# A Mamba-2 block with eight LoRA experts on one NeuronCore: turning h and B by VectorE squares and DRAM in place of TensorE transposes

## The chip, the cores and the metric

The kernel runs on one NeuronCore of a Trainium2 chip. A core has TensorE (PE in the profile), VectorE (DVE), ScalarE (ACT), GpSimd (POOL) and SyncE (SP), which here issues every DMA. The metric is the device time of one execution in microseconds (us). The kernel before took 1603.26 us, the median of three runs (1601.43 to 1604.12).

## The reference

The input x has 1024 rows (time steps) of 512. It is normalised, and three things are added up: x, a Mamba-2 block of the normalised x, and a dense layer with a top-2 mixture of eight rank-16 LoRA experts.

```python
proj = einsum('bsd,ed->bse', xn, in_proj_w)          # gate 8192, hBC 10240, dt 128
hBC  = silu(causal_conv4(hBC) + conv_b)              # hs: 128 heads x 64; B, C: 8 groups x 128
dt   = clip(softplus(dt + dt_bias), 0, 100)
xch  = hs * dt                                       # in chunks of 128 steps
A_cum = cumsum(dt * -exp(A_log))                     # in each chunk
Y_diag = einsum('bzlhn,bzshn,bhzls,bzshp->bzlhp', C, B, L, xch)    # L = exp(segsum), lower triangle
states = einsum('bzlhn,bhzl,bzlhp->bzhpn', B, decay_states, xch)   # handed on from chunk to chunk
Y_off  = einsum('bzlhn,bzhpn,bhzl->bzlhp', C, prev, exp(A_cum))
g = (Y_diag + Y_off + hs * D) * silu(gate)
out = einsum('bsi,oi->bso', group_rms_norm(g) * norm_w, out_proj_w)
```

All is float32. Large products are computed as three matmuls of numbers split in a high and a low part (hi x hi, hi x lo, lo x hi).

## The kernel before

**Stage 1.** The normalised x lies turned in SBUF (channels on partitions, time along the row) as xh and xl. The 18,432 output channels of the projection, and the 128 of dt, are computed in 145 blocks of 128 channels by 1024 steps. `block` (L664) loads a weight (wr, 256 KB), splits it (ACT makes wh, POOL makes wl, `split` L323), and `project` (L407) runs 24 matmuls of 128x512 into two PSUM banks (pp_r). ACT and DVE take these out: a gate block through Silu, the others through four conv taps (L685, L694) and Silu (L697). Results have channels on partitions.

The scan works on units of four heads, that is, two blocks of h (`scan`, L739; 32 units, four to a group). Some products need time on partitions, so h and B have to be turned:

- `group` (L706) turns B by 8 PE transposes (bt, L718), from whose PSUM banks ACT and DVE make the split parts bh and bl (L720, L722). It also makes cbm, the masked product of C and B (cb, L732).
- `scan` turns each of the two h blocks by 8 PE transposes in two halves of time (hT, L776). DVE multiplies each half by dt (xdt, L778), POOL by the decay (xf, L784), and ACT and POOL split that (xdh L789, xdl L791).
- Three matmuls per chunk make the states' increments (ps, L802); DVE runs the recurrence over chunks (st, L809 and L813).
- For each head a row of A_cum is loaded to all partitions (L, 512 KB); ACT and DVE make of it the decay matrix (L758, L760, L762). Two products of half the array's width follow: yo from st and C (L837), y from xdt and L (L849). DVE and POOL combine them with h, D and the gate (L841 to L859), and the result is stored in DRAM (g_d).

**Stage 2.** The experts and the dense layer (`ffn`, L507; pp_rt, pp_la, pf) stand between; then the gated result is loaded again by time (gr), split, and multiplied with the output weights (po, L920); the norm is applied to the sums (L941).

**Order.** No loop of the source sets the order of instructions. Every operation is handed to a planner (`Plan`, L98) with an engine, a duration, what it reads and writes, and an urgency: its unit's number plus an offset from the table URGE. The planner plays the engines through and gives each engine, when free, the ready operation with the lowest number, and each buffer a place when it is first needed. CAPS says how many buffers of a kind may live at once; PSUM is eight banks shared by the kinds mm, ts and yy. For PE it also charges changes between the kinds of matmul (SHORT, LONG, HALVES for y and yo, MIDDLE for ps). Instructions are then written in that order, and every engine, and SP with its DMAs, executes its own in order.

Of the kernel before, what the change touches and what calls it, by code (L numbers as in the profile page):

```python
# [8 lines left out]
F32 = mybir.dt.float32  # L9
FR = mybir.dt.float32r  # L10
AF = mybir.ActivationFunctionType
ALU = mybir.AluOpType
# [37 lines left out]
URGE = dict(w=9.24, part=-0.279, proj=-0.002, evac=-1.876, silu=-2.632, group=-0.486, hT=0.407, xdt=2.385, xf=-1.176,  # L50
            split=-0.323, ps=-2.368, st=-1.089, Ll=-7.231, Lr=6.458, Le=2.863, Lm=5.964, el=-2.393, yo=0.086,
            tt=-1.918, y=3.42, yt=-3.901, out=1.039, switch=2.019, short=0.042, long=0.133, halves=-1.335,
            middle=-3.841, leave=2.869, c0=36.517, c=0.019, ffn=32.348, rt=-5.457, la=-0.436, early=-6.249,
            hold=0.232, gate=-0.092, w0=79.012)
CAPS = dict(hs=5, gate=15, ct=2, L=7, e=2, xdt=25, wr=3, wh=3, wl=8, y=4, tt=2, xf=2, mm=13, ts=3, yy=17)
# [42 lines left out]
class Plan:  # L98
# [33 lines left out]
    def run(self):  # L132
# [11 lines left out]
        while left:  # L144
            began = False
            soon = 1e30
            for e in ENGINES:
# [4 lines left out]
                for o in todo[e]:  # L152
                    same = e == "PE" and o.mode == mode == HALVES
                    if o.ready > t + 1e-9:
                        soon = min(soon, o.ready)
                        stay |= same and o.ready < t + URGE["hold"]
                        continue
# [3 lines left out]
                    if e == "PE" and o.mode != mode:  # L161
                        urge += URGE[("short", "long", "halves", "middle")[o.mode]]
                        if mode == HALVES:
                            urge += URGE["leave"]
# [10 lines left out]
                    for k, bs in wanted.items():  # L175
# [12 lines left out]
                        if ready[many[pool] - 1] > t + 1e-9:  # L188
                            soon = min(soon, ready[many[pool] - 1])
                            stay |= same and ready[many[pool] - 1] < t + URGE["hold"]  # L190
                            good = False
                            break
# [50 lines left out]
def block_kernel(ctx, tc, x, in_w, conv_w, conv_b, dt_bias, A_log, Dv, norm_w, out_w,  # L243
# [10 lines left out]
    def ctile(shape, name, dt=F32):  # L254
# [19 lines left out]
    elast_d = dram.tile([H, NZ], F32, name="elast_d")  # L274
    g_d = [dram.tile([BPG, P, S], F32, name=f"g_d{g}") for g in range(G)]
# [5 lines left out]
    big, wide, small = Pool("big", 30, 1024, sb), Pool("wide", 3, 1792, sb), Pool("small", 15, 512, sb)  # L281
    K = {n: Kind(big, CAPS.get(n, 1)) for n in ("hs", "gate", "bT", "ct", "cbm", "bh", "bl", "L", "e", "xdt", "dts", "As",
                                                "dec", "eA")}
# [19 lines left out]

    def halves(h):
        return slice(h * HALF, (h + 1) * HALF)
# [11 lines left out]
    XH, XL = new("xh", "xh", S, FR), new("xl", "xl", S, FR)  # L317
    G_D = [thing(f"g_d{g}") for g in range(G)]
# [18 lines left out]
    op("PE", 6.0, warm_up(12), w=[warm], urge=-9.0)  # L337
# [5 lines left out]
    for n, what in enumerate((0, 1, wdt, 2, 3, w0, 4, 5, 6, 7)):  # L343
        lag, urge = 2.64 + (0.3, 0.38)[n > 2] * n + 0.1 * (n > 2), -8.0 + 0.001 * n
# [16 lines left out]
    split(*wdt, -7.3)  # L361
# [45 lines left out]
    def project(w, acc, half, urge, take=(), quarters=False):  # L407

        for q in range(2) if quarters else ():
            def go(q=q):  # L410
                n, c = 0, slice(q * 256, q * 256 + 256)
                hi, lo = w[0](), w[1]()
                for a, b in ((hi, XH()), (hi, XL()), (lo, XH())):
                    for k in range(NK):
                        pe.matmul(acc()[:, c], a[:, k, :], b[:, k, halves(half)][:, c], start=n == 0, stop=n == 11)
                        n += 1
            mk = 3 << 4 * half + 2 * q
            op("PE", 1.44, go, r=[w[0], w[1], (XH, mk), (XL, mk)], w=[(acc, 1 << q)], urge=urge,
               take=take if q == 0 else (), mode=LONG)
# [244 lines left out]
    def block(u, i, row, ci, kind, name):  # L664
# [3 lines left out]
        if row:  # L668
            dma(raw, lambda: in_w[row], 3.6, w=[raw], urge=urge + URGE["w"])
            split(raw, hi, lo, urge + URGE["part"])  # L670
# [34 lines left out]

    def group(g, u):  # L706
# [5 lines left out]
        for hf in range(2):  # L712
            zs = slice(hf * 4, hf * 4 + 4)
            acc = new("mm", f"bt{g}_{hf}", P)

            def turn(acc=acc, hf=hf):
                for z4 in range(4):
                    pe.transpose(acc()[:, z4, :], gr.B()[:, zsl(hf * 4 + z4)], ident)  # L718
            op("PE", 0.436, turn, r=[gr.B], w=[acc], urge=urge, take=[gr.bh, gr.bl] if not hf else ())
            op("ACT", 0.49, lambda acc=acc, zs=zs: act.activation(gr.bh()[:, zs, :], acc(), AF.Copy), r=[acc],  # L720
               w=[(gr.bh, zmask(hf))], urge=urge)
            op("DVE", 0.6, lambda acc=acc, zs=zs: dve.tensor_tensor(  # L722
                gr.bl()[:, zs, :], acc(), f32(gr.bh()[:, zs, :]), ALU.subtract), r=[acc, (gr.bh, zmask(hf))],
                w=[(gr.bl, zmask(hf))], urge=urge)
# [14 lines left out]
    def scan(u, hs, gate):  # L739
# [24 lines left out]
        for j in range(2):  # L764
            b = 2 * u + j
            cols = slice(j * P, (j + 1) * P)
            for hf in range(2):
                tp = new("ts", f"hT{b}_{hf}", P)
                n = 4 - hf
                zs4, zs = slice(hf * 4, hf * 4 + 4), slice(hf * 4, hf * 4 + n)  # L770
                mk = zmask(hf)
                late = 0.02 * (2 * j + hf)

                def turn(tp=tp, hf=hf, j=j):
                    for z4 in range(4):
                        pe.transpose(tp()[:, z4, :], hs[j]()[:, zsl(hf * 4 + z4)], ident)  # L776
                op("PE", 0.436, turn, r=[hs[j]], w=[tp], urge=at("hT") + late, take=[xdt[j]] if not hf else ())
                op("DVE", 0.6, lambda tp=tp, j=j, b=b, zs4=zs4: dve.tensor_tensor(  # L778
                    xdt[j]()[:, zs4, :].rearrange("p z (a c) -> p z a c", a=2),
                    tp().rearrange("p z (a c) -> p z a c", a=2),  # L780
                    dts()[:, zs4, 2 * b:2 * b + 2].unsqueeze(3).to_broadcast([P, 4, 2, 64]), ALU.mult),
                    r=[tp, dts], w=[(xdt[j], mk)], urge=at("xdt") + late)
                xf = new("xf", f"xf{b}_{hf}", shape=[P, n, P])
                op("POOL", 1.0 if n == 4 else 0.8, lambda xf=xf, j=j, b=b, zs=zs, n=n: pool.tensor_tensor(  # L784
                    xf().rearrange("p z (a c) -> p z a c", a=2),
                    xdt[j]()[:, zs, :].rearrange("p z (a c) -> p z a c", a=2),
                    dec()[:, zs, 2 * b:2 * b + 2].unsqueeze(3).to_broadcast([P, n, 2, 64]), ALU.mult),
                    r=[(xdt[j], mk), dec], w=[xf], urge=at("xf") + late, port=True)
                op("ACT", 0.54 if n == 4 else 0.44, lambda xf=xf, zs=zs, cols=cols: act.activation(  # L789
                    xdh()[:, zs, cols], xf(), AF.Copy), r=[xf], w=[(xdh, mk << 8 * j)], urge=at("split") + late)  # L790
# [200 lines left out]
```

## Time and profile before

| | us |
|---|---|
| median of three runs (lowest, highest) | 1603.26 (1601.43, 1604.12) |
| the profiled execution | 1604.36 |
| its span, first to last instruction | 1602.7 |
| PE projection matmuls (pp_r, L426), share of the chain | 45% |
| PE output matmuls (po, L920), share of the chain | 22% |
| PE hT (L776), share of the chain | 3% |
| DVE xdt from PSUM (L778), 128 of 512 wide | 80.2 busy, 683 ns each |
| ACT table loads, 203 in all | 1283 ns each |
| DMA, mean over the span | 143 GB/s, 229.98 MB |

The profile comes from one execution, and its times are compared with that execution's own. "Busy" is time in which an engine has an instruction running; on PE these records overlap. The chain is found from the last instruction backwards: at each step to what released it, or to the instruction before it on its engine. The granted clock (PEclk) is 1.00 after the first 50 us.

### The profile page before, as it was taken

How to read it: one execution, taken by the hardware profiler on the slowest of the kernel's cores; microseconds unless marked ns; L12 is line 12 of the kernel's file. 1: busy time of each engine (PE TensorE's matmuls, PEld its weight loads, DVE VectorE, ACT ScalarE, POOL GpSimd, SP SyncE). 2: the span in 40 equal slices, each digit the busy share in tenths (PEclk: the TensorE clock that was granted, in tenths of full speed). 3: DMA queues.
4: the chain of work that ended last, by engine and by line, in shares of the span. 5: the costliest groups of instructions: out<-in, count | busy, mean ns of one | idle time of the engine just before them, and what ended most of it. 6: DMA issues, size and time to landing. Idle time of an engine off the chain costs nothing.

```text
span 1602.7 us, 28828 instructions
## 1 busy us (share of the span) xinstructions
PE 1592.1 (99%) x10616; PEld 1355.2 (85%) x10616; DVE 1282.2 (80%) x2209; ACT 1294.4 (81%) x2275; POOL 832.9 (52%) x768
## 2 busy tenths in 40 slices
PE   8999999999999999999999999999999999999999
PEld 8888888888888888888888888888887888888887
DVE  6798987786888788777878877787788788888874
ACT  6899989997999899799989988998973554444531
POOL 3269757847775776678576847866755000000000
PEclk9999999999999999999999999999999999999999
DMA  4534725444443555344344615544545655554512
GB/s 132 186 105 155 244 89 175 136 136 135 148 154 117 172 158 162 108 161 155 116 138 146 204 66 157 183 155 129 155 135 173 169 139 156 158 142 127 138 55 72
DMA packets 140605, 229.98 MB, mean 143 GB/s; under 512 B 11056, under 2 KB 76720, under 8 KB 140464
## 3 DMA queue, kind: packets, MB, share of 16 engines
q1 hardware_dynamic: 140464, 228.14, 46.5%
q8 instruction: 84, 1.38, 0.4%
q14 instruction: 57, 0.47, 0.1%
HBM read 191.39 MB, written 36.70 MB: 142 GB/s over the span
## 4 chain that ended last, share of the span: by engine, by line
PE 93%; POOL 3%; ACT 2%; issue 1%; DMA 0%; DVE 0%; SPq 0%; POOLq 0%; DVEq 0%
PE pp_r L426 45%; PE po L920 22%; PE y L849 7%; PE yo L837 6%; PE ps L802 5%; PE hT L776 3%; PE pf L652 1%; PE cb L732 1%; POOL yt L856 1%; POOL xdl L791 1%; POOL xf L784 1%; ACT L L758 1%; POOL g L859 1%; PE bt L718 0%; PE vp L932 0%
## 5 line engine op out<-in xcount | busy, mean ns | idle before, releaser
L426 PE MATMUL pp_r<-xh,wh 128*128 128x512 f32 x1144 | 454.2, 397 | 0.0
L426 PE MATMUL pp_r<-xh,wl 128*128 128x512 f32 x1144 | 446.3, 390 | 1.3 <-POOL wl L325 1.3
L426 PE MATMUL pp_r<-xl,wh 128*128 128x512 f32 x1144 | 446.4, 390 | 0.0
L694 DVE SCALAR_TENSOR_TENSOR h<-pp_r,cw,h 128x512 f32<-128x512 f32 (+2 forms) x384 | 283.3, 748 | 73.7 <-ACT h L685 67.7
L758 ACT ACTIVATE L<-L,As 128x128 f32<-128x128 f32 x1024 | 319.4, 391 | 0.0
L325 POOL TENSOR_TENSOR wl<-wr,wh 128x512 fp32r<-128x512 f32 x144 | 192.4, 1340 | 208.3 <-ACT wh L324 182.8
L426 PEld LDWEIGHTS pp_r<-xh,wl 128*128 128x128 f32 x1144 | 214.8, 188 | 48.3 <-POOL wl L325 2.2
L426 PEld LDWEIGHTS pp_r<-xh,wh 128*128 128x128 f32 x1144 | 215.0, 188 | 45.7 <-issue 3.9
L426 PEld LDWEIGHTS pp_r<-xl,wh 128*128 128x128 f32 x1144 | 215.2, 188 | 41.0
L762 DVE TENSOR_TENSOR L<-L,cbm 128x1024 f32<-128x1024 f32 x128 | 189.0, 1493 | 52.5 <-ACT L L760 52.1
L910 ACT ACTIVATE gr<-gr 128x1024 f32<-128x1024 f32 x64 | 67.8, 1060 | 157.6 <-DVE gl L908 157.6
L856 POOL TENSOR_TENSOR yt<-yt,tt 128x384 f32<-128x384 f32 (+1 forms) x128 | 157.3, 1240 | 68.8 <-DVE yt L853 60.4
L859 POOL TENSOR_TENSOR g<-yt,g 128x512 f32<-128x512 f32 x128 | 185.2, 1458 | 3.1
L791 POOL TENSOR_TENSOR xdl<-xf,xdh 128x512 fp32r<-128x512 f32 (+1 forms) x128 | 152.3, 1198 | 28.1 <-ACT xdh L789 28.1
L784 POOL TENSOR_TENSOR xf<-xdt,dec 128x512 f32<-128x512 f32 (+1 forms) x128 | 131.8, 1040 | 55.8 <-DVE xdt L778 55.6
L813 DVE SCALAR_TENSOR_TENSOR st<-st,eA,ps 128x64 f32<-128x64 f32 x768 | 151.4, 276 | 1.1
L911 DVE TENSOR_REDUCE sq<-gr 128x128 f32<-128x1024 f32 x64 | 128.7, 2013 | 19.1 <-ACT gr L910 19.0
L760 ACT ACTIVATE L<-L 128x1024 f32<-128x1024 f32 x128 | 135.6, 1059 | 1.5
L920 PE MATMUL po<-owh,gh 128*128 128x512 f32 x512 | 128.9, 394 | 0.0
L778 DVE TENSOR_TENSOR xdt<-hT,dts 128x512 f32<-128x512 f32 x128 | 80.2, 683 | 59.7 <-PE hT L776 59.7
L920 PE MATMUL po<-owh,gl 128*128 128x512 f32 x512 | 126.5, 389 | 0.0
L920 PE MATMUL po<-owl,gh 128*128 128x512 f32 x512 | 126.5, 389 | 0.0
(175 smaller groups left out, 2806.1 us busy)
## 6 DMA issues: line engine op xcount, KB each, us to landing
L<-acum_d SPq DMA_DIRECT2D x128, 512.0 KB, 5.8
wr<-in_w SPq DMA_DIRECT2D x144, 256.0 KB, 2.8
g_d<-g SPq DMA_DIRECT2D x64, 512.0 KB, 4.6
gr<-g_d SPq DMA_DIRECT2D x64, 512.0 KB, 6.7
e<-exp_d SPq DMA_DIRECT2D x128, 224.0 KB, 6.3
ow<-out_w SPq DMA_DIRECT2D x64, 256.0 KB, 3.6
x<-x SPq DMA_DIRECT2D x8, 256.0 KB, 5.3
acc<-x SPq DMA_DIRECT2D x8, 256.0 KB, 4.3
```

The costliest lines, as they stand in the source:

```text
L325: op("POOL", dur[1], lambda: pool.tensor_tensor(lo(), raw(), f32(hi()), ALU.subtract), r=[raw, hi], w=[lo], urge=urge, port=True)
L426: pe.matmul(acc(), a[:, k, :], b[:, k, halves(half)], start=n == 0, stop=n == 11)
L694: dve.scalar_tensor_tensor(d, acc()[:, :n], cw[:, ci, k:k + 1], d, ALU.mult, ALU.add)
L758: act.activation(L()[:, z, :], L()[:, z, :], AF.Relu, bias=As()[:, z, h:h + 1], scale=-1.0)
L760: op("ACT", 0.97, lambda L=L: act.activation(L(), L(), AF.Exp, scale=-1.0), w=[L], urge=at("Le") + 0.05 * a, table="exp")
L762: op("DVE", 1.14, lambda L=L: dve.tensor_tensor(L(), L(), gr.cbm(), ALU.mult), r=[gr.cbm], w=[L], urge=at("Lm") + 0.05 * a, port=True)
L784: op("POOL", 1.0 if n == 4 else 0.8, lambda xf=xf, j=j, b=b, zs=zs, n=n: pool.tensor_tensor(xf().rearrange("p z (a c) -> p z a c", a=2), x ...
L791: op("POOL", 1.24 if n == 4 else 0.96, lambda xf=xf, zs=zs, cols=cols: pool.tensor_tensor(xdl()[:, zs, cols], xf(), f32(xdh()[:, zs, cols] ...
L813: dve.scalar_tensor_tensor(st()[:, z, c], st()[:, z - 1, c], eA()[:, 4 * u + a, z:z + 1], pt()[:, z % 2, c], ALU.mult, ALU.add)
L856: op("POOL", 1.25 if n == 4 else 0.97, lambda yt=yt, tt=tt, part=part: pool.tensor_tensor(yt()[:, part], yt()[:, part], tt()[:, part], ALU ...
L859: op("POOL", 1.24, lambda yt=yt, j=j, hf=hf: pool.tensor_tensor(gate[j]()[:, halves(hf)], yt(), gate[j]()[:, halves(hf)], ALU.mult), r=[yt ...
L920: pe.matmul(po(), a()[:, b, :], wts[g, b // per][k]()[:, b % per, :], start=n == 0, stop=n == 23)
```

## The change

In the changed kernel no transposes of h and B are made on PE. A new function `turn` does it: DVE's transpose instruction turns each 32x32 square of a 128x1024 block, four DMAs store the result in one of four 512 KB places in DRAM so that the squares change their partitions, and one DMA loads it back. ACT and DVE then read bh and bl, and xdt, from this SBUF tile (moved), not from PSUM. xdt, xf, xdh and xdl are now cut by head (64 columns, all eight chunks) and no longer by half of time, and ps and y wait for whole tiles.

The buffers are shared out anew (34 large ones in place of 30), the urgencies are new, the planner's charge for a change of matmul kind becomes a table of pairs, the loads at the start stand in another order, and the first projections are handed over in smaller pieces. A reserve for DMAs issued by GpSimd, which the kernel has none of, is cut to 512 bytes.

```diff
-CAPS = dict(hs=5, gate=15, ct=2, L=7, e=2, xdt=25, wr=3, wh=3, wl=8, y=4, tt=2, xf=2, mm=13, ts=3, yy=17)
+CAPS = dict(hs=4, gate=4, ct=2, L=6, e=4, xdt=9, turned=5, wr=4, wh=3, wl=9, y=2, tt=1, xf=4, mm=5, ts=9, yy=5)
...
                     if e == "PE" and o.mode != mode:
-                        urge += URGE[("short", "long", "halves", "middle")[o.mode]]
-                        if mode == HALVES:
-                            urge += URGE["leave"]
+                        urge += URGE["SLHM"[mode] + "SLHM"[o.mode]]
...
+    turn_d = [dram.tile([4, 32, 4, 256], F32, name=f"turn_d{i}") for i in range(4)]
...
-    big, wide, small = Pool("big", 30, 1024, sb), Pool("wide", 3, 1792, sb), Pool("small", 15, 512, sb)
+    big, wide, small = Pool("big", 34, 1024, sb), Pool("wide", 3, 1792, sb), Pool("small", 15, 512, sb)
...
+    def turn(src, name, at, urge):
...
+        turned, moved = new("turned", f"T{name}"), new("moved", f"M{name}")
+
+        def store():
+            for q in range(4):
+                sp.dma_start(turn_d[at][q].rearrange("r i f -> i r f"), turned()[:, 256 * q:256 * q + 256])
+        op("DVE", 1.12, lambda: dve.transpose(
+            turned().rearrange("p (q z c) -> p z q c", q=4, z=NZ), src().rearrange("p (z q r) -> p z q r", q=4, z=NZ)),
+            r=[src], w=[turned], take=[moved], urge=urge)
+        op("SP", 1.8, store, lag=4.6, r=[turned], w=[TURN_D[at]], urge=urge)
+        dma(lambda: moved().rearrange("p (i f) -> p i f", i=4), lambda: turn_d[at].rearrange("q r i f -> (q r) i f"),
+            5.0, r=[TURN_D[at]], w=[moved], urge=urge)
+        return moved
...
-                    pe.transpose(acc()[:, z4, :], gr.B()[:, zsl(hf * 4 + z4)], ident)
...
+        moved = turn(gr.B, f"B{g}", g % 4, urge)
...
+        op("ACT", 1.05, lambda: act.activation(*both(moved, gr.bh)[::-1], AF.Copy), r=[moved], w=[gr.bh],
+           take=[gr.bl], urge=urge)
+        op("DVE", 1.15, lambda: dve.tensor_tensor(both(moved, gr.bl)[1], both(moved, gr.bl)[0],
+                                                  f32(both(moved, gr.bh)[1]), ALU.subtract),
+           r=[moved, gr.bh], w=[gr.bl], urge=urge, port=True)
...
-                    for z4 in range(4):
-                        pe.transpose(tp()[:, z4, :], hs[j]()[:, zsl(hf * 4 + z4)], ident)
-                op("PE", 0.436, turn, r=[hs[j]], w=[tp], urge=at("hT") + late, take=[xdt[j]] if not hf else ())
...
+            moved = turn(hs[j], f"h{b}", b % 4, at("hT") + late)
+            for a in range(2):
...
+                op("DVE", 0.6, lambda j=j, a=a, h=h, moved=moved: dve.tensor_tensor(
+                    xdt[j]()[:, :, 64 * a:64 * a + 64].rearrange("p z (i c) -> p z i c", i=2),
+                    flat4(moved).rearrange("p i (z c) -> p z i c", z=NZ)[:, :, 2 * a:2 * a + 2, :],
+                    dts()[:, :, h:h + 1].unsqueeze(2).to_broadcast([P, NZ, 2, 32]), ALU.mult),
+                    r=[moved, dts], w=[(xdt[j], 1 << a)], urge=at("xdt") + late, port=True)
+                xf = new("xf", f"xf{b}_{a}", shape=[P, NZ - 1, 64])
...
-            op("PE", 0.36 * len(zz), products, r=[(gr.bh, mk & 255), (gr.bl, mk & 255), (xdh, mk), (xdl, mk)], w=[pt],
+            op("PE", 0.36 * len(zz), products, r=[(gr.bh, mk), (gr.bl, mk), xdh, xdl], w=[pt],
...
-                op("PE", 0.875, diag, r=[(xdt[j], zmask(hf)), *((M[i], zmask(hf)) for i in (range(4) if j == 0 else (2, 3)))], w=[yp],
+                op("PE", 0.875, diag, r=[xdt[j], *((M[i], zmask(hf)) for i in (range(4) if j == 0 else (2, 3)))], w=[yp],
```

The turn's buffers: turned may live five times at once, moved once (it has no entry in CAPS, and the default is 1); it is taken with the DVE instruction and given back after the last read.

## The prediction

> **What bounds the kernel now.** I read the busy times and the chain of work that ended last, then the busy time by stage, then stretches of TensorE's timeline.
>
> ```profile
> PE 1592.1 (99%) x10616; PEld 1355.2 (85%) x10616; DVE 1282.2 (80%) x2209; ACT 1294.4 (81%) x2275; POOL 832.9 (52%) x768
> ...
> PE 93%; POOL 3%; ACT 2%; issue 1%; DMA 0%; DVE 0%; SPq 0%; POOLq 0%; DVEq 0%
> ```
>
> The last line is the chain: 93% of the span is work of TensorE (PE). Busy records of pipelined matmuls overlap, so below I price by the distance between starts. By stage (the length, then busy us of PE, weight loads, VectorE, ScalarE, GpSimd, then granted clock, DMA share, GB/s):
>
> ```profile
> 0.00:1242.00 1242.00, 1235.38 (x9015) 1060.74 (x9016) 997.10 (x1930) 1131.39 (x2079) 832.90 (x768) 1.00 0.47 148
> 1242.00:1603.00 361.00, 356.76 (x1602) 294.49 (x1600) 285.11 (x279) 163.04 (x197) 0.00 (x0) 1.00 0.46 128
> ```
>
> Stage 1 (projections and scan) holds everything that changes. PE has no room in it; ACT is at 91%, DVE at 80%, POOL at 67%. In stage 2 (the output projection) no instruction changes, and I cost it at 0. PE's idle time over the span is 1602.7 - 1592.1 = 10.6 us, and the table of 50 us windows has 4.7 of it in the first 50 us and about 4 at the end: some 2 us are left for all waits between.
>
> **Removed from TensorE.** The built program of the changed kernel has none of the 512 hT and 64 bt transposes. One visit of 16 among projection matmuls (start, length):
>
> ```profile
> 603.27 0.40 PE L426 MATMUL pp_r<-xh,wl 128*128 128x512 f32 x1
> 603.50 1.91 PE L776 MATMUL hT<-ident,h 128*128 128x128 f32 x16
> 605.17 0.47 PE L426 MATMUL pp_r<-xh,wh 128*128 128x512 f32 x1
> 605.48 0.39 PE L426 MATMUL pp_r<-xl,wh 128*128 128x512 f32 x1
> ```
>
> From 603.27 to 605.48 are 2.21 us, in which two projection matmuls stand at their pace of 0.227 (603.27 to 603.50): the visit costs 1.756 us, 0.110 a transpose. 576 of them are **63 us** (576 x 1.67/16 = 60 without the slow restart).
>
> The Trainium skill, page "VectorE: DVE Perf Modes", section "The three transpose paths", gives 390 ns for a 128x128 transpose on TensorE and 311 on VectorE (bf16), and its rules for authors send 128x128 transposes to TensorE; an estimate from that page would be 576 x 0.39 = 225 us off PE and 72 x 8 x 0.311 = 179 us onto DVE. The trace's 0.110 us between starts speaks against using the first figure as a pace; no run so far shows the second.
>
> **Moved on TensorE.** The order is new, and in the built programs I counted how often PE goes from other work to the half-width matmuls of y and yo: 43 times before, mostly one visit of 120 matmuls per unit; 140 times after, by 12 to 44. A short visit of before:
>
> ```profile
> 98.66 0.39 PE L426 MATMUL pp_r<-xh,wl 128*128 128x512 f32 x1
> 98.98 1.09 PE L837 MATMUL yo<-C,st 128*64 128x128 f32 x16
> 100.00 0.50 PE L426 MATMUL pp_r<-xh,wh 128*128 128x512 f32 x1
> 100.34 0.40 PE L426 MATMUL pp_r<-xl,wh 128*128 128x512 f32 x1
> ```
>
> 98.66 to 100.34 less two slots of 0.227 is 1.226 us for 16 matmuls, while 16 inside a long visit take 0.87 in the chain:
>
> ```profile
> 592.12 0.87 PE y L849 x16
> ```
>
> A visit costs 0.35 us of its own, at entry (0.32 for 0.227) and exit (0.34 for 0.227). 97 more are **+34 us**; so the new order gives back half of the gain. Nine fewer visits to the ps matmuls (41 to 32), at about 0.11 each by the same reckoning, are -1. PE in sum: -63 + 34 - 1 = **-30 us**, stage 1 at 1212.
>
> **Added to VectorE.** 72 turns of 128x1024 in 32x32 squares. No row shows one. Below, two tensor_scalars of 512 (L466, 0.42 each) give 0.85; above, the strided reduction over 1024 takes 2.01 (L911). I take 1.20, nearest to the plain 1024-wide operation:
>
> ```profile
> L762 DVE TENSOR_TENSOR L<-L,cbm x128: 1208/1246/2348, 73.7 to 1186.6; 128x1024 f32<-128x1024 f32 x128
> ```
>
> That is 86 us (61 to 145). The xdt products now read SBUF twice, not PSUM once (0.683 mean): from half of L762's minimum, 0.60, to that plus L762's own excess of mean over minimum (1.493 - 1.208), 0.89; that is -11 to +26 over 128, and I take +15. bl is the same amount in half as many instructions: 0. DVE in stage 1: 997 + 86 + 15 = **1098 us**, 91% of 1212 (1047 to 1168 at the ends).
>
> The page "SBUF — State Buffer", section "SBUF: two separate sides", says that a VectorE operation with two SBUF inputs and a GpSimd one that reads SBUF exclude each other for a whole instruction. L762's maximum of 2348, one 1.1 us block over its minimum, agrees; if all 128 xdt products waited for half of a 1.3 us GpSimd instruction, an estimate by that rule, they would cost +83 us in place of +15.
>
> **Added wait.** The turned tile goes to DRAM in four stores and back in one load, and only one returned buffer may live (moved has the default cap 1). So DVE does turn, other work, xdt products, next turn, one after another, 72 times; in 45 places the next turn stands right behind a product in DVE's queue, and the L products, conv taps and later y (PE) wait behind it. On SP the load waits for the stores; in 43 of 72 turns nothing stands between, and next in the queue is mostly a weight load, which the projections need. Up to nine split weights may be kept ready, so I cost that at 0. The round trip: three further issues at 0.33, a store and a load.
>
> ```profile
> L<-acum_d SPq DMA_DIRECT2D x128, 512.0 KB, 5.8
> wr<-in_w SPq DMA_DIRECT2D x144, 256.0 KB, 2.8
> g_d<-g SPq DMA_DIRECT2D x64, 512.0 KB, 4.6
> gr<-g_d SPq DMA_DIRECT2D x64, 512.0 KB, 6.7
> ```
>
> Low: 1.0 + 2.6 (acum_d's store) + 2.8 + 0.2 for handing over = 6.6. High: 1.0 + 6.7 + 6.7 + 0.2 = 14.6. I take g_d's and L's rows: 1.0 + 4.6 + 5.8 + 0.2 = **11.6 us**. Other DMAs then add 75.5 MB to stage 1 (72 x 1.05), about 210 GB/s for 148, so the low end is unlikely.
> The cover is what DVE executes between a turn and its first product; summed in the new order with the durations of the rows it is 11.8 us on average, under 9 in a tenth of the turns, over 15 in another. Stalls summed over 72 turns by round trip: 32 us at 10, 83 at 11.6, 146 at 13, 195 at 14. At 11.6 DVE has 1098 + 83 = 1181 us of 1212: still inside, barely.
>
> **The rest.** ACT has 203 table loads before, 187 after: 16 x 1.283 = -20.5, so 1111 of 1212, 92%; it lies beside PE and gains nothing. POOL has the same number of operations. SP issues 360 more DMAs, 119 us at 0.33, beside everything. The start (load order, split projections) can gain at most the 4.7 us of idle there or lose as much: 0. Fewer buffers (gate 15 to 4, xdt 25 to 9, banks shared out anew) execute nothing, but absorb less delay. For that and DVE's tightness I put four times PE's 2 us of waits: **+8**, where 0 and 40 (half of the 83 us reaching PE) are the ends.
>
> **Sum** on the profiled execution (1604.4, of it 1602.7 span; 1.1 over the median of 1603.3): 1604.4 - 30 + 8 = **1582 us**.
>
> **Rivals.** Changes under 0.2% (1600 to 1606.5) can't be told from none.
> - Forecast, 1570 to 1597: PE stays the bound. For it: PE's queue was all but gapless with ACT at 91%. Against: DVE at 91%, the serial turn. **0.58.**
> - The visits' price is hidden, or fewer switches show than counted: 1604.4 - 64 + 8 = 1548. Against: every short visit in the trace shows the price. **0.05.**
> - DVE and PE level: with a round trip of 12.4, stalls of 117 make DVE 1215; both then wait for one another, say +25 in place of +8, 1599. **0.18**, of it 0.07 inside 1600 to 1606.5.
> - Slower: the one returned buffer makes DVE the bound. It decides from a round trip of 13 us (1098 + 146 = 1244, stage 1 as long as before); at 14 the stage is 1293 and the time 1655. For it: each DMA competes with more of its kind, and e's 224 KB already take 6.3 us. Against: 11.6 from medians. **0.19.**
> That the transposes stay on PE is excluded by the count.
>
> Faster 0.58 + 0.05 + 0.11 = 0.74, same 0.07, slower 0.19. The range 1566 to 1615 leaves out the second case and most of the last, about 0.2.
>
> **What would show it.** Right: no hT rows; PE busy near 99% of stage 1, ending near 1212 to 1225; y/yo visits with 0.32 and 0.34 at their edges; turn near 1.2 us; xdt 0.7 to 0.9; DVE about 90%. Wrong: DVE's idle time ended by the returned tile's DMA, above 110 us in all, or round trips of 13 us and more; PE idle with y or ps waiting for DVE; visits cheaper than 0.35.

## The result, and the profile after

The changed kernel takes **1753.89 us** (median of four runs, 1752.65 to 1761.35) where the kernel before takes 1602.78 (four runs, 1601.43 to 1604.12): a ratio of 1.0952, 95% interval 1.0920 to 1.0985. The forecast of 1582 was wrong in sign and missed by 172 us. The profiled execution took 1761.35 us, its span is 1759.2.

First the busy times and the chain, from the page of the changed kernel:

```profile
PE 1630.3 (93%) x10042; PEld 1325.0 (75%) x10042; DVE 1384.8 (79%) x2273; ACT 1278.8 (73%) x2251; POOL 873.9 (50%) x768
...
PE 21%; DMA 3%; DVE 1%; ACT 1%; SPq 0%; issue 0%; POOL 0%; DVEq 0%; ACTq 0%; POOLq 0%
```

No engine is full any more: PE fell from 99% to 93%, and nobody took its place. (The shares of the chain sum to 26%: it could be followed back to 1262 us only, through stage 2 and the end of stage 1.) By stage, with the columns as before (length, then PE, weight loads, VectorE, ScalarE, GpSimd, granted clock, DMA share, GB/s):

```profile
0.00:1396.00 1396.00, 1271.36 (x8411) 1029.04 (x8411) 1094.24 (x1990) 1115.43 (x2054) 864.09 (x762) 0.95 0.58 184
1396.00:1759.00 363.00, 358.93 (x1634) 295.92 (x1632) 290.52 (x284) 163.41 (x197) 9.84 (x7) 1.00 0.49 134
```

Stage 2 is as long as before (363 us for 361), so all of the loss lies in stage 1: 1396 us for 1242. There PE stands idle for 125 us, and its granted clock is 0.95. Up to the last matmul the clock is halved in 23 stretches of 3.4 to 13.7 us, 140 us together. PE is idle in 34 of these anyway and works in 106, which is worth 53 us of full-speed work; before it was 3. The forecast's sum was 1574 without waits; the profiled execution is 187 above it. Idle time grew by 118 us (6.6 to 125) and the work lost to the clock by 50 (3 to 53): **168 of the 187**. So the PE work itself came out within 19 us of the forecast, and most of the error is time in which PE waited, or ran at half clock in or after a wait.

Who waited for whom, from the table of waits (us in total, times, longest):

```profile
POOL xf L795 <- DVE xdt L789: 187.1, 67, 9.8
...
DVE xdt L789 <- DMA Mh<-turn_d: 118.9, 45, 6.5
ACT xdh L800 <- POOL xf L795: 115.4, 55, 6.4
...
ACT L L774 <- DMA L<-acum_d: 41.1, 18, 6.7
PE ps L813 <- ACT xdh L800: 39.0, 13, 7.1
...
PE ps L813 <- POOL xdl L802: 30.8, 25, 2.9
```

DVE waits 45 times for the returned tile, POOL for DVE, ACT for POOL, and PE's ps matmuls for ACT and POOL. The line of ACT and L is another path: the rows of A_cum (L) come late as well, though the change does not touch them. SyncE's own queue tells why:

```profile
SPq L326 <- DMA turn_d<-Th: 373.0, 108, 7.9
SPq L716 <- DVE Th L717: 196.2, 37, 9.0
...
SPq L326 <- DMA turn_d<-TB: 55.2, 16, 6.3
```

SP stands 373 us for the stores of turned tiles of h (and 55 more for those of B), up to 7.9 us at a time; everything later in its one stream of DMAs stands with it. One stretch of that stream (start, length):

```profile
619.78 2.29 SPq L716 DMA_DIRECT2D turn_d<-Th  x4
623.83 0.33 SPq L326 DMA_DIRECT2D wr<-in_w  x1
628.41 0.33 SPq L326 DMA_DIRECT2D Mh<-turn_d  x1
628.79 2.23 SPq L326 DMA_DIRECT2D L<-acum_d  x2
```

The four stores are issued by 622.07. The load is next but one, and goes out at 628.41, 6.3 us after them; two L rows are behind it. Over the 72 turns (medians from the trace): the four issues 2.3 us, from the last of them to the load's issue 6.7, from there to the first reader 3.9, in all **13.5 us**.

The clock, at one place. The first fence is PE's timeline, the second the busy times of the stretches around it:

```profile
508.20 0.28 PE L813 MATMUL ps<-xdh,bl 128*128 128x256 f32 x1
511.06 0.39 PE L813 MATMUL ps<-xdl,bh 128*128 128x256 f32 x1 [2.58 <-POOL xdl L802]
```

```profile
500.00:512.00 12.00, 9.31 (x68) 7.57 (x67) 9.15 (x13) 8.41 (x13) 10.01 (x9) 1.00 0.74 235
512.00:519.00 7.00, 5.43 (x21) 4.55 (x20) 5.54 (x23) 6.66 (x16) 1.65 (x4) 0.51 0.22 76
```

PE waits 2.58 us for a split that POOL makes late, and from 512.2 on the clock is at half for 6.8 us. That is up to 3.4 us of work lost, so here a short wait costs more than its own length.

### The profile page after: what moved, and what is told of

Read it like the earlier page. It is cut to its first block, busy times and chain, and to the rows that moved or that the text cites. A ratio compares the mean times of both kernels' runs of the same rounds, so it can differ in the third digit from the quotient of the medians.

```text
span 1759.2 us, 28363 instructions
## 1 busy us (share of the span) xinstructions
PE 1630.3 (93%) x10042; PEld 1325.0 (75%) x10042; DVE 1384.8 (79%) x2273; ACT 1278.8 (73%) x2251; POOL 873.9 (50%) x768
## 5 line engine op out<-in xcount | busy, mean ns | idle before, releaser
L429 PE MATMUL pp_r<-xh,wh 128*128 128x512 f32 x1144 | 470.6, 411 | 14.6 <-ACT wh L329 10.2
L429 PE MATMUL pp_r<-xh,wl 128*128 128x512 f32 x1144 | 453.6, 396 | 13.7 <-POOL wl L330 13.7
L429 PE MATMUL pp_r<-xl,wh 128*128 128x512 f32 x1144 | 453.4, 396 | 0.0
L330 POOL TENSOR_TENSOR wl<-wr,wh 128x512 fp32r<-128x512 f32 x144 | 197.5, 1378 | 151.9 <-ACT wh L329 80.1
L795 POOL TENSOR_TENSOR xf<-xdt,dec 128x448 f32<-128x448 f32 x128 | 140.6, 1111 | 190.9 <-DVE xdt L789 187.1
L789 DVE TENSOR_TENSOR xdt<-Mh,dts 128x512 f32<-128x512 f32 x128 | 98.8, 799 | 123.3 <-DMA Mh<-turn_d 118.9
L802 POOL TENSOR_TENSOR xdl<-xf,xdh 128x448 fp32r<-128x448 f32 x128 | 172.1, 1357 | 32.2 <-ACT xdh L800 32.0
L800 ACT ACTIVATE xdh<-xf 128x448 fp32r<-128x448 f32 x128 | 72.2, 571 | 115.5 <-POOL xf L795 115.4
L848 PE MATMUL yo<-C,st 128*64 128x128 f32 x1792 | 131.6, 281 | 10.4 <-DVE st L824 10.0
L848 PEld LDWEIGHTS yo<-C,st 128*64 128x64 f32 x1792 | 98.8, 137 | 56.3 <-issue 30.5
```

The lines of the kernel that those rows point to most:

```text
L330: op("POOL", dur[1], lambda: pool.tensor_tensor(lo(), raw(), f32(hi()), ALU.subtract), r=[raw, hi], w=[lo], urge=urge, port=True)
L429: pe.matmul(acc(), a[:, k, :], b[:, k, halves(half)], start=n == 0, stop=n == 11)
L795: op("POOL", 0.9, lambda xf=xf, j=j, a=a, h=h: pool.tensor_tensor(xf(), xdt[j]()[:, :NZ - 1, 64 * a:64 * a + 64], dec()[:, :NZ - 1, h:h + ...
L802: op("POOL", 1.1, lambda xf=xf, cols=cols: pool.tensor_tensor(xdl()[:, :, cols], xf(), f32(xdh()[:, :, cols]), ALU.subtract), r=[xf, (xdh, ...
L848: pe.matmul(yo()[64 * a:64 * a + 64, zsl(z4)], st()[:, z - 1, c:c + 64], gr.C()[:, zsl(z)], start=True, stop=True)
```

## The experiments

The time of the kernel before, on the same chip, was between 1601.5 and 1605.0 us in every comparison. The theory I began with: the loss is the round trip, for which VectorE waits and SyncE stands. The rivals: the one returned buffer; the new order by itself; the added traffic.

### Without one wait or the other

In the first run xdt reads h as it is, not the returned tile, so that VectorE no longer waits; h's values are then unturned and the output is not the reference's.

```diff
-                    flat4(moved).rearrange("p i (z c) -> p z i c", z=NZ)[:, :, 2 * a:2 * a + 2, :],
+                    flat4(hs[j]).rearrange("p i (z c) -> p z i c", z=NZ)[:, :, 2 * a:2 * a + 2, :],
```

> The changed kernel, but the xdt products read h itself and not the returned tile (so they use unturned values); turns, stores, loads, their places in every queue and SP's waits stay, only DVE no longer waits for h's round trip (B's 8 trips stay). Theory A (DVE stands at xdt until the trip of about 13.5 us is over, and the one returned buffer makes trips serial): the 119 us of DVE waiting for the load go, PE's waits at ps shrink, time 1590 to 1650. Theory B (SP stands for the landing of the stores, 428 us in all, and weights and L rows queued behind come late): time stays above 1720. Theory C (the new order and the smaller buffer counts are bad by themselves): time stays above 1700.

In the second the load fetches rows of x in place of the stored tile, so that it need not wait for the stores (the turned values are not used).

```diff
-        dma(lambda: moved()..., lambda: turn_d[at].rearrange("q r i f -> (q r) i f"),
+        dma(lambda: moved()..., lambda: x.rearrange("(p a) f -> p (a f)", p=P)[:, :1024].rearrange("p (i f) -> p i f", i=4),
```

> The changed kernel with the same order and the same bytes, but the load brings back a part of the input x of the same shape from DRAM and not the turned squares (so xdt, bh and bl get other values): it no longer waits for the stores, and nor does SP. The trip from turn to product falls from 13.5 us to some 6.5. Theory A: within 20 us of the run in which xdt reads h. Theory B: this run is lower than that one by 60 us or more, near 1600. Theory C: above 1700.

Then both edits together, and then a kernel with the same order in which h's stores and loads are left out altogether (xdt reads unturned h; B's trips stay):

```diff
-            for q in range(4):
+            for q in range(4) if name[0] == "B" else ():
...
+            if name[0] == "B":
+                sp.dma_start(moved()..., turn_d[at].rearrange("q r i f -> (q r) i f"))
```

> Both edits: the load takes a part of x and waits for no store, and the xdt products read h itself (other values for xdt, bh and bl). Order, instructions and bytes as in the changed kernel. What is above 1602 here is neither DVE's nor SP's wait for a trip. Expected 1640 to 1665, little under the run without the wait for the stores; if DVE's 50 us of waiting there counted in full, 1610 to 1625.

> h is still turned by VectorE, but its stores and loads are left out and the xdt products read h itself (other values); B's trips stay; the order of all other instructions is the same. Theory D (the 67 MB of h's trips, in the queue ahead of L, e and the weights, cost the rest): 1570 to 1600, PE near its sum of 1574. Theory C (the new order, and DVE at 90%): 1640 or more, as in the run without waits.

Measured: without VectorE's wait **1701.64**, without SyncE's **1666.43**, without both **1629.98**, without h's traffic **1613.17**. Against 1753.9 these are -52, -87, -124 and -141. All four lie between the ranges set for them beforehand (the first is 2 us inside theory C's "above 1700"): each wait is a part of the loss and neither is all of it. The second run does not remove SyncE's wait alone, for VectorE's went from 118.9 to 50.1 us with it:

```profile
DVE xdt L789 <- DMA Mh<-x: 50.1, 22, 5.4
```

With VectorE's wait already gone, SyncE's is worth 72 us (1701.6 to 1630.0), and VectorE's without SyncE's 36 (1666.4 to 1630.0). SyncE's standing, which the prediction had put at nothing, is the larger of the two. In the second run the loads no longer wait, yet where VectorE waited for them they took some 8.0 us from issue to reader, in place of 3.8: they now run beside the stores (and read rows of x).

### More returned buffers

```diff
-CAPS = dict(hs=4, gate=4, ct=2, L=6, e=4, xdt=9, turned=5, ...)
+CAPS = dict(hs=4, gate=4, ct=2, L=6, e=4, xdt=9, moved=3, turned=5, ...)
```

> The changed kernel with three returned buffers allowed (moved=3 in CAPS), so that the planner may overlap turns; it still believes in trips of 9.6 us. Theory A: the chain of 72 trips is cut, 1620 to 1690, with DVE's wait for the load below 60 us. Theory B: no gain, 1740 or more, since each load still holds SP. Theory C: 1700 or more.

The same with the measured landing times in the planner's costs:

```diff
-        op("SP", 1.8, store, lag=4.6, r=[turned], w=[TURN_D[at]], urge=urge)
+        op("SP", 2.4, store, lag=9.4, r=[turned], w=[TURN_D[at]], urge=urge)
...
-            5.0, r=[TURN_D[at]], w=[moved], urge=urge)
+            3.9, r=[TURN_D[at]], w=[moved], urge=urge)
```

> Three returned buffers, and the planner is told what the trace shows: four stores take SP 2.4 us and land after 9.4, the load lands after 3.9. Theory A: DVE has other work over each trip, wait for the load below 20 us, 1580 to 1640. Theory B: better than the three buffers alone by 30 us or more, because SP's waits are now planned too. Theory C: 1680 or more, the numbers of urgency and the other counts being as in the changed kernel.

Measured: **1799.92** and **1747.59**, against 1620 to 1690 and 1580 to 1640 of the theory that more buffers help; it fell. With three buffers the trips overlap and lengthen (medians of some 15 and 17 us). But the planner made a new order in both runs, so they do not yet clear the one returned buffer, my slower rival's mechanism; a run in the changed kernel's own order does that below. I looked next at the transfers.

### The order without the trip

The changed kernel's urgencies and buffer counts, with the turns on PE as before (the planner makes an order of its own from them, with 146 visits to the half-width matmuls for 140):

```diff
-            moved = turn(hs[j], f"h{b}", b % 4, at("hT") + late)
...
+                    for z4 in range(4):
+                        pe.transpose(tp()[:, z4, :], hs[j]()[:, zsl(hf * 4 + z4)], ident)
```

> The changed kernel's planner, urgency numbers and buffer counts, but h and B are turned by TensorE and cut by half of time as before: no turns, no trips; the order is what the planner makes of that, and PE has the 63 us of transposes again. Theory C (the new numbers and counts are bad by themselves): 1680 or more. If the turns and their trips are the whole loss: PE's sum of before plus the dearer visits, 1600 to 1650.

Measured: **1648.23**, 43 us over the kernel before on the same chip (1605.02).

```profile
PE 1632.2 (99%) x10618; PEld 1345.9 (82%) x10618; DVE 1278.5 (78%) x2209; ACT 1250.1 (76%) x2236; POOL 844.5 (51%) x768
```

PE is full; there are 146 visits in place of the 43 of before. 103 x 0.35 = 36 us of the 43 are what the prediction's price gives. The new urgencies and counts cost about what the prediction said of the new order.

### One store of whole lines

```diff
-            for q in range(4):
-                sp.dma_start(turn_d[at][q].rearrange("r i f -> i r f"), turned()[:, 256 * q:256 * q + 256])
+            sp.dma_start(turn_d[at], turned())
...
+            for q in range(4):
+                sp.dma_start(moved()[32 * q:32 * q + 32, :].rearrange("r (i f) -> r i f", i=4),
+                             turn_d[at][:, 256 * q:256 * q + 256].rearrange("(i r) f -> r i f", i=4))
```

> The same trip cut the other way: one store of 4 KB lines, then four loads that pick 1 KB pieces for 32 partitions each; order as planned with the store at 0.45 us of SP. If the 7 us from the last store's issue to its landing come of the 1 KB lines of the stores, the trip falls to about 10 us and the time to 1680 to 1720. If a trip is as long whichever side is cut, 1740 to 1770.

Measured: **1685.37**. VectorE's wait for the load fell to 2.8 us and the store landed some 2.8 us after its issue, but half of the loss stayed. I read that as "half of it is not the store". It was a misreading: I had also given the planner a cheaper store and a dearer load (0.45 and 1.8 us), and it made another order, in which SP stood for the turns themselves:

```profile
SPq L715 <- DVE Th L721: 339.9, 64, 11.8
```

An edit that goes through a planner is two changes. From here on I changed the DMAs inside an operation and left its planned cost alone, so that the order stayed the same.

### The same order, three ways to store

With the short trip, urgencies, buffers and the planner's landing times were chosen anew twice (order3 with nine returned buffers, order4 with five), and the changed kernel's own stores were put into order4.

```diff
-CAPS = dict(hs=4, gate=4, ct=2, L=6, e=4, xdt=9, turned=5, wr=4, wh=3, wl=9, y=2, tt=1, xf=4, mm=5, ts=9, yy=5)
+CAPS = dict(hs=4, gate=5, ct=2, L=8, e=2, xdt=14, moved=5, turned=11, wr=3, wh=3, wl=13, y=4, tt=3, xf=3, mm=5, ts=8, yy=11)
```

> The short trip of the store_whole run (one store of 4 KB lines, four loads) with the order's urgencies and the buffers chosen anew for it (nine returned buffers instead of one, 99 half-width visits instead of 140). Computes everything. Theory (the loss is visits plus waits for the trip, each of them avoidable): the PE sum falls by 41 visits x 0.35 = 14 us, from 1574 to 1560, and the 111 us that store_whole stood above the sum fall to the 39 that were left with h's traffic left out: 1585 to 1620. Rival (the trip costs the engines something by itself, whatever the order): still some 110 above the sum, 1650 to 1680.

> As the run beside it with another choice of urgencies and buffers: 74 half-width visits, five returned buffers, eleven turned ones. Computes everything. Theory (visits plus avoidable waits): PE sum 1574 - 66 x 0.35 = 1551, and some 20 to 50 above it: 1570 to 1600, so as fast as the kernel before or up to 2% faster. Rival (the trip costs by itself): 110 above the sum, 1650 to 1670.

> The same instructions in the same order and buffers as whole_order4, with the changed kernel's own trip: four stores of 1 KB lines and one load instead of one store of 4 KB lines and four loads. Computes everything. Theory (the stores of 1 KB lines land some 4 us later and SP, whose stream is in order, stands for them 72 times): 40 to 130 us slower than whole_order4, 1630 to 1700, with SP's wait for the stores as its largest. Rival (only the order and the buffers matter): within 15 us of whole_order4.

Measured: order3 **1619.84** (ratio 1.0105, 1.0086 to 1.0124), order4 **1600.96** (0.9984, 0.9969 to 0.9998), order4 with the cut stores **1764.56**. One edit to the DMAs, in the same order, costs 164 us, more than expected.

The cut stores differ in two ways: their lines are of 1 KB, not 4, and their pattern in DRAM ("i r f") has 4 as its outermost size. (One load takes the place of four as well.) The trace's count of landing signals points to the second. Before, 635 DMAs give 10,160 signals, 16 each. In the changed kernel 995 DMAs give 12,752, which is 707 x 16 + 288 x 5; with the whole stores 995 give 15,920, 16 each. The 288 stores of turned tiles are the only DMAs that signal 5 times.

The Trainium skill, page "DMA: Bandwidth & Descriptors", section "Why a DMA increments its semaphore by 16 and not by 1", says that a DMA is spread over the largest number of engines up to 16 that divides the outermost size (other than 1) on both sides, and that the issuing sequencer itself makes up the missing signals at once. By that rule a store with 4 outermost runs on 4 of 16 engines, and five signals are four engines' and the sequencer's. The counts agree. At the 27 GiB/s an engine of the page's "Specifications", 128 KB through four is an estimate of 1.1 us, 4.5 for four stores.

The packets in the trace agree. In the changed kernel those of 1 KB, 512 a turn, are all the stores': in 78% of the time in which any is under way there are four or five at once, and a turn's run 6.7 us from the first to the last (medians of 72 turns), most of the wait. The measurement is above the estimate of 4.5.

To tell line from engines, the same order once more, again with stores of 1 KB lines, but 128 outermost:

```diff
-                sp.dma_start(turn_d[at][q].rearrange("r i f -> i r f"), turned()[:, 256 * q:256 * q + 256])
+                sp.dma_start(turn_d[at][q], turned()[:, 256 * q:256 * q + 256])
```

> The order and buffers of whole_order4 and cut_order4. Again four stores of 1 KB lines per turn, as in cut_order4, but each to a place in DRAM of its own whose access pattern has 128 as its outermost size, not 4 (the squares are permuted by the four loads). Computes everything. In the traces the cut stores signal their landing 5 times each, every other DMA 16 times. Theory A (the cut stores are slow because each is carried by only 4 of the 16 DMA engines): they land about as fast as the whole store, some 3 to 4 us after the last issue, and the time is 1600 to 1640, the three further issues of 0.3 us on SP costing a little. Theory B (lines of 1 KB are slow by themselves): the load still waits 6 to 7 us after the last store, and the time is 1730 or more.

Measured: **1598.03**, with 1,211 DMAs and 19,376 signals, 16 each. SP's wait for h's stores, in order4 with 4 engines and then with 16:

```profile
SPq L716 <- DMA turn_d<-Th: 313.9, 100, 7.4
```

```profile
SPq L717 <- DMA turn_d<-Th: 22.3, 19, 3.0
```

The line's length makes no difference here; A holds, 2 us under its range, and B is out. The pair differs further in where the lines lie in DRAM and in its loads: each of the four waits for its own store alone, so the first mostly goes out before the last store has landed. But in order4 with the whole store the loads wait for all of it, and that run takes 1601. And until the load goes, ten or more packets of the stores are under way at once in 57% of the time in which any is, with the cut stores never more than eight. So it is the number of engines that decides the wait.

### The changed kernel's own order, on all 16 engines

The decisive run: the changed kernel with its own order, urgencies and one returned buffer; the stores as just above, and four loads that permute the squares, under the load's old planned cost.

```diff
-        dma(lambda: moved()..., lambda: turn_d[at].rearrange("q r i f -> (q r) i f"),
-            5.0, r=[TURN_D[at]], w=[moved], urge=urge)
+        def fetch():
+            for q in range(4):
+                sp.dma_start(moved()[32 * q:32 * q + 32, :].rearrange("r (i f) -> r i f", i=4),
+                             turn_d[at][q].rearrange("(i r) f -> r i f", i=4))
+        op("SP", 0.45, fetch, lag=5.0, r=[TURN_D[at]], w=[moved], urge=urge)
```

> The changed kernel with its own order, urgencies and buffers (one returned buffer), where only the trip's DMAs are cut otherwise: the four stores go to places whose outermost size is 128 and so use all 16 DMA engines, and four loads permute the squares. Computes everything. Theory A (the four-engine stores cost the changed kernel what its new order does not): the round trip falls from 13.5 to about 8 us, the waits for it on VectorE (118.9) and SyncE (428) to under a quarter, the time to 1613 to 1690, nearer to the low end (the run without h's traffic, 1613) if nothing else is in the way. Theory C (the one returned buffer and the tight order keep the loss whatever the stores take): within 40 us of the changed kernel, 1710 or more.

Measured: **1611.45**, 142 us less than the changed kernel, 2 under the range of theory A, and as fast as with h's traffic left out (1613). C is out. From the first store's issue until the load has landed a trip takes 7.9 us, in place of 12.8. The busy times, then two waits, then the landing times of the trip's DMAs (count, KB each, us from issue to landing):

```profile
PE 1577.0 (98%) x10042; PEld 1290.4 (80%) x10042; DVE 1394.1 (87%) x2273; ACT 1275.7 (79%) x2251; POOL 882.0 (55%) x768
```

```profile
DVE xdt L793 <- DMA Mh<-turn_d: 15.6, 9, 3.5
```

```profile
SPq L724 <- DMA turn_d<-Th: 20.6, 22, 2.1
```

```profile
turn_d<-Th SPq DMA_DIRECT2D x256, 128.0 KB, 1.9
Mh<-turn_d SPq DMA_DIRECT2D x256, 128.0 KB, 3.0
```

VectorE's wait went from 118.9 to 15.6 us, SP's from 373.0 to 20.6, PE's idle time in stage 1 from 125 to 28, the halved clock from 140 to 24 us. The one buffer and SP's in-order stream are still there, so neither is a cause by itself.

### By which way the four engines cost, and a better order

Two things were open: whether an order that expects the late store covers it, and whether the turn through DRAM can beat the kernel before. order5 is chosen for landing times near those of order4 (e 8.0, L 7.3, weights 4.4 us), with the whole store; order6 for stores that land 6.9 us after their issue. Both have fifteen returned buffers, and beside the urgencies (further counts differ too):

```diff
-CAPS = dict(hs=4, gate=5, ct=2, L=8, e=2, xdt=14, moved=5, turned=11, ...)
+CAPS = dict(hs=4, gate=5, ct=2, L=8, e=2, xdt=15, moved=15, turned=6, ...)      # order5
+CAPS = dict(hs=4, gate=5, ct=2, L=8, e=2, xdt=17, moved=15, turned=10, ...)     # order6
```

> The trip with one whole store and four loads (all 16 engines) in a further order, whose planner is told the landing times that the run whole_order4 showed (e 8.0, L 7.3, weights 4.4 us); 80 half-width visits. Computes everything. Theory (what whole_order4 keeps above its PE sum are waits for loads that land later than its planner was told, at the start above all): PE sum 1574 - 60 x 0.35 = 1553 and 15 to 40 above it, 1568 to 1593, faster than before by 0.6 to 2%. Rival (VectorE at 88% and the tight chain POOL, ACT, PE keep some 50 whatever the planner is told): 1598 to 1610.

> The order and buffers of whole_order5 with four stores of 1 KB lines on all 16 engines in place of the whole store. Computes everything. In order4 this pair gave 1601 and 1598, so within 8 us of whole_order5 either way; SyncE's wait for the stores falls to a fifth (125 to 22 us in order4) and its issues take 72 x 1.5 us more.

> The changed kernel's own four stores (4 of 16 engines) and one load, in an order made for a store that lands 6.9 us after its issue: fifteen returned buffers, 98 half-width visits. Computes everything. Theory A (the price of the late landing is that SyncE and VectorE stand for it, and an order that expects it can cover it): PE sum 1574 - 42 x 0.35 = 1559 and 20 to 60 above, 1580 to 1620. Theory B (the four engines are a bound of their own: 72 stores through 4 engines hold up every other transfer's share there, in any order): 1680 or more.

> The order and buffers of four_order6 with the stores on all 16 engines and four loads. Computes everything. If the order covers the late store, this is within 20 us of four_order6; if not, it is 60 or more below it, near the runs of order4: 1575 to 1605.

Measured: order5 with the whole store **1594.81** (ratio 0.9949, 0.9934 to 0.9964), between the theory's 1593 and the rival's 1598; with 1 KB lines on 16 engines 1598.42 (0.9976, 0.9966 to 0.9985); order6 with four engines **1711.94**, with sixteen **1638.34** (1.0224, 1.0207 to 1.0241). An order that expects the late store does not cover it: 74 us remain between the last two, and SP still stands 179 us for the stores. Theory B of that run is nearer, but this pair does not part "the four engines hold up every other transfer" from "the landing is too late to plan for". order6 itself was worse than I expected of it (1575 to 1605), so it is no good witness of how well a late store can be covered.

Other runs do so in part. With five signals counted for a four-engine store and 16 for every other DMA, the landings can be read from the traces. Transfers that the change does not touch do land later beside the four-engine stores: in the changed kernel the weights after 5.6 us, L after 7.9 and e after 7.5, against 4.0, 5.9 and 4.8 in the same order on 16 engines (medians). But the run without both waits, its stores still on four engines and its weights landing after 7.1 us, took 1630, 18.5 us more than 1611. So of the 142 us some 124 go when neither SP nor VectorE stands for h's trip; what the late other transfers add while SP stands is not told apart.

order5 with the whole store is the fastest kernel of this study, 0.5% under the kernel before:

```profile
PE 1555.5 (98%) x10042; PEld 1299.5 (82%) x10042; DVE 1415.0 (89%) x2273; ACT 1220.4 (77%) x2210; POOL 857.9 (54%) x768
```

It has 80 half-width visits in place of 140 and 31 us of PE idle time left in stage 1.

## Why the prediction was wrong

**The loss in parts.** The new urgencies and buffers cost 43 us (1648.2 against 1605.0, turns on PE). Taking the turns off PE with them gains 37 (1648.2 to 1611.5, stores on 16 engines; the planner's order differs between these two). The stores on 4 engines cost 142 (1611.5 to 1753.9, the same order). The parts sum to the whole by the way they are taken, 149 us over the 1605.0 of the first; against the median of before it is 151. The last part is most of the error. But without it the kernel is still 10 us slower than the one before (1611.5 against 1601.9 in that comparison), not 21 faster as forecast.

**PE's sum: right, to within 19 us.** No transposes are left, and idle time with the clock explains 168 of the 187 us over 1574. The price of a visit holds: from the changed kernel's timeline,

```profile
617.18 0.39 PE L429 MATMUL pp_r<-xh,wl 128*128 128x512 f32 x1
617.50 1.09 PE L848 MATMUL yo<-C,st 128*64 128x128 f32 x16
618.52 0.50 PE L429 MATMUL pp_r<-xh,wh 128*128 128x512 f32 x1
618.86 0.40 PE L429 MATMUL pp_r<-xl,wh 128*128 128x512 f32 x1
```

0.32 at entry and 0.34 at exit, and 1.68 us from the first row to the last, as predicted. (The two edges account for 0.21 of the 0.35; the rest lies inside the visit, 1.02 us for 0.87.)

**VectorE: right.** The groups (busy us, mean ns):

```profile
L789 DVE TENSOR_TENSOR xdt<-Mh,dts 128x512 f32<-128x512 f32 x128 | 98.8, 799 | 123.3 <-DMA Mh<-turn_d 118.9 <-issue 4.5
...
L717 DVE STREAM_TRANSPOSE Th<-h 128x1024 f32<-128x1024 f32 x64 | 79.0, 1234 | 1.2 <-ACT h L700 1.2
```

A turn takes 1.234 us (forecast 1.20), an xdt product 0.799 (0.80), and VectorE is busy 1094 us in stage 1 (1098). ScalarE: 1115 (1111). The prediction's two estimates from pages come out too high: 72 turns take 89 us on VectorE for 179, and the products cost 19 us more than before (98.8 for 80.2) where waiting for GpSimd would have made it 83.

**The round trip: the failed step.** "I take g_d's and L's rows: 1.0 + 4.6 + 5.8 + 0.2 = 11.6." The sum was 1.9 us short of the 13.5 measured, and the nearness is luck, for its parts were wrong in opposite directions: stores 9.0 us (2.3 to issue, 6.7 to land) where I had 5.6, load 3.9 where I had 6.0. The rows I took were of DMAs that signal 16 times. The stores of the change are not of that kind, and the diff says so: `rearrange("r i f -> i r f")` puts a 4 outermost. On 16 engines the same stores are issued in 1.8 us and have all landed 1.4 us later. I had not asked whether the new DMAs resemble the rows that priced them.

**SyncE's waiting: the step that cost most.** "Up to nine split weights may be kept ready, so I cost that at 0." SP stood 428 us in all, and behind it were not only weights: L rows, e rows and the next turns' stores were late too. Taking that wait away gained 72 us where VectorE's was gone already, and 87 together with half of VectorE's; VectorE's alone gained 52.

**The waits: +8, with 40 as the end; measured +187.** I tied PE's loss to VectorE's stall alone and took half of it. But waits on different engines (SP, DVE, POOL, ACT) followed one another down to PE, and PE's 41 gaps of over 1 us brought 23 stretches at half clock, which no step of mine had.

**The slower rival: right in sign and in its threshold, not in its mechanism.** It was to decide from a round trip of 13 us; it was 13.5. But that is luck: between its stalls of 146 and 195 us, 13.5 gives a stage 1 of some 1270 us, and 1396 were measured. VectorE did not become the bound (1094 busy and 119 waiting, of 1396 us), and with the one buffer still there the stores on 16 engines removed the loss. The range's upper end of 1615 is the sum with 40 us of waits, from VectorE's stall alone.

What stays open: how much of the 142 us comes by other transfers that land late while SP stands; and what keeps the repaired kernel 37 us over PE's sum, of which idle time and clock give 28.

## What to carry to other kernels

Before a new DMA is priced by a row of the profile, compare its access pattern with that row's, outermost size first: from the first store's issue until all four had landed it took 9.0 us on 4 engines and 3.3 on 16, and the kernel 1754 us or 1611. A wait in SP's one stream is never beside other work unless everything behind it is early; count what is behind it. Where a planner orders the instructions, change an operation's inside and leave its planned cost alone, or the run tells of two changes.

## What had not been expected of the hardware

- The four-engine stores and their count of signals, as told above.
- The clock. The Trainium skill, page "TensorE: Matmul & The Clock Gate", section "Why this matters for your kernels", asks for no idle gaps above some 3 us between bursts. Here 14 of the 23 half-clock stretches of the changed kernel follow gaps that are all shorter than 3 us (longest gap that reaches into the 4.2 us before the stretch: 1.28 to 2.91); four more begin 2.1 to 3.0 us after the start of a longer gap. The measurement decides: gaps of one to three us cost clock too, though not each of them (41 gaps over 1 us, 23 stretches).
- A load issued right behind the four-engine stores (of rows of x) took some 8.0 us to the reader that waited for it, 3.8 when it (then of the turned tile) was issued after they had landed.
